# A four-layer graph network on one core: the gated layer's difference on GpSimd, and softmax sums by a 129th operand column

## The chip, the cores and the metric

The kernel runs on one core of a Trainium2 chip. The metric is the device time of one execution in microseconds (us); a lower one is better. The engines are called PE (TensorE, matrix products), PEld (its weight loads), DVE (VectorE), ACT (ScalarE), POOL (GpSimd) and SP (SyncE, which issues transfers here).

## What is computed

The input x is 64 graphs of 256 nodes with 128 features; adj is one 256x256 matrix that all graphs share. Four layers follow one another. Each normalises its input over the features, clips it at zero, and adds its result to the input. Layer 0 is a gated recurrence of five steps, layer 1 a sum of node mixings with adj and its square, layer 2 one mixing with a row norm, layer 3 an attention over node pairs:

```python
# layer 0, five times
u3 = h @ u3_w.T + u3_b
z = sigmoid(av @ w3_w.T + w3_b + u3)
r = sigmoid(av @ w4_w.T + w4_b + u3)
hv = tanh(av @ w5_w.T + w5_b + (r * h @ u5_w.T + u5_b))
h = (1.0 - z) * h + z * hv
# layer 3
pre = s1[:, :, None, :] + s2[:, None, :, :] + b_lin
h = where(pre >= 0, pre, 0.2 * pre)
e = einsum('bije,e->bij', h, a) + bias
attn = softmax(e, axis=2)
out = sigmoid(einsum('bij,bjf->bif', attn, x))
```

Here av holds adj times h twice, and in layer 3 the weights W and the bias are adj itself. Everything is in 32-bit floats.

## The kernel before

**Pairs, fronts, tiles, tails.** Two graphs form a pair (32 pairs), so that a tile [128, 2, 256] has 512 elements in each partition. For each pair a "front" (from L391) works through layers 0 to 2 and the start of layer 3: it is one long dependent chain, in which products run on PE, the Tanh and the copies out of PSUM on ACT, elementwise work on DVE, and the small inverse roots on POOL. Sigmoids are written with Tanh.

The large work is layer 3's pairwise sum and its clipping. It is cut into 128 "tiles" a pair (4096 in all), each of 128x2048 elements and called rl. A tile can be made on any of three engines: on DVE by one instruction (L703), on ACT by eight (L716), on POOL by eight (L723). DVE's tiles belong to one half of the hidden features, POOL's to the other, ACT makes either. PE scores each tile with two groups of four matmuls, once for each of the two passes of a 32-bit product (L760; each record in the profile is one of these). 13 rl tiles are in turn use.

When all 64 tiles of a block of 128 nodes have been scored, a "tail" (two for each pair) does the softmax and the weighted sum: DVE adds adj (L609), POOL adds a row term (L613, the sum sc+lin over 128x512 elements), DVE takes the negated maximum (L617), ACT takes Exp with an accumulated output as the softmax sum (L622; the accumulator is read out by an instruction of its own), PE transposes, ACT copies with a factor 0.5 to wT (L631), PE multiplies by h3, DVE inverts the sums (L643), ACT takes Tanh with that scale into o (L648), POOL finishes (L652, L653), and SP sends the result out.

**Order.** No engine chooses at run time. A planner in the kernel keeps a clock for each engine and plays the whole program through while it is being built: `ran(engine, us, ...)` advances a clock by a duration written in the code, and `yield ENGINE, since` in a front or tail says which engine has the next step and from when. At each point the engine that is free first takes a step of a tail, else of a front, else a part of a tile. What it takes is then fixed as that engine's program order, each instruction depending on the one before it. On POOL a part of a tile is two instructions, on ACT four, on DVE the whole tile. So a change in any step or duration moves the order on all engines, and also how many tiles each makes. Fronts are spread so that about two of them are under way at any time. Buffers with `tag="short"` come from a ring of 12, the tiles hT from a ring of 4, and three PSUM banks are lent out by `take()` and given back through `spare`.

**The steps that the change touches.** In a step of layer 0, pr and pv are PSUM banks with sums. ACT takes Tanh of pr for z (L437), and Tanh of pv in place, in PSUM (L440). Then:

```python
            yield DVE, t
            d = feat("d", **SHORT)
            nc.vector.tensor_sub(d, by_feature(pv[0]), hT)
            t = ran(DVE, ELEMENTS, t)
            spare.append([pv[0], t])
            yield DVE, max(t_z, clock[DVE])
            nc.vector.scalar_tensor_tensor(by_feature(pr[0]), by_feature(pr[0]), 1.0, d, op0=OP.add, op1=OP.mult)
```

These are L445 (the difference d, 160 times: 32 pairs by 5 steps) and L449 (the product); L453 forms the new hT. The norms (L365 to L376) go from DVE through POOL (L299, L300, L372) to ACT. In layer 3, h3 is the normalised input, tokens in partitions, that the weighted sum reads.

Of the kernel before, what the change touches and what calls it, by code (L numbers as in the profile page):

```python
# [8 lines left out]
F32 = mybir.dt.float32  # L9
AF = mybir.ActivationFunctionType  # L10
# [4 lines left out]
P = 128  # L15
NB = 2
# [4 lines left out]
PE, DVE, ACT, POOL = ENGINES = (mybir.EngineType.PE, mybir.EngineType.DVE, mybir.EngineType.Activation, mybir.EngineType.Pool)  # L21
# [4 lines left out]
def kernel(  # L26
# [50 lines left out]
    nc = tc.nc  # L77
    B, N, D = x.shape
    NC = N // P
# [5 lines left out]
    work = ctx.enter_context(tc.tile_pool(name="work", bufs=2))  # L85
# [9 lines left out]
    clock = dict.fromkeys((PE, DVE, ACT, POOL), 0.0)  # L95
# [4 lines left out]
    def ran(engine, us, *after):  # L100
        start = max(clock[engine], 0.0, *after)
        if engine == ACT:
            behind[0] = max(0.0, behind[0] - (start - clock[ACT])) + 0.024 * us
        clock[engine] = start + us
        return clock[engine] + SEEN[engine] + (behind[0] if engine == ACT else 0.0)
# [6 lines left out]
    spare = [[b, 0.0] for b in banks[5:]]  # L112
# [6 lines left out]
    def by_feature(b):  # L119
        return b.rearrange("p (b n) -> p b n", b=NB)  # L120

    def by_token(b):
        return b.rearrange("p (b c n) -> p b c n", b=NB, c=NC)
# [29 lines left out]
    ident = const.tile([P, P], F32, name="ident")  # L153
# [43 lines left out]
    bz, br, bh = gate_b[:, 0:1], gate_b[:, 1:2], gate_b[:, 2:3]  # L197
# [123 lines left out]
    def to_feature(pt, h):  # L321

        pt = by_token(pt)
        for b in range(NB):
            for c in range(NC):
                nc.tensor.transpose(pt[:, b, c, :], h[:, b, c, :], ident)

    def to_token(pt, ht):

# [16 lines left out]
    def tok(name, **kw):  # L346
        return work.tile([P, NB, NC, D], F32, name=name, **kw)

    def rows_of(t):
        return t.rearrange("p b c d -> p (b c) d")  # L350
# [5 lines left out]
    COPY, BIASED, TANH, ELEMENTS = 0.48, 0.58, 0.57, 0.61  # L356

    def norm(src, since, h):

        stats = work.tile([P, NB * NC, 6], F32, name="stats")  # L360
        mv = work.tile([P, NB * NC, 2], F32, name="mv")
        s, h = rows_of(src), rows_of(h)
        yield DVE, since
        for k in range(NB * NC):
            nc.vector.bn_stats(stats[:, k, :], s[:, k, :])  # L365
        for k in range(NB * NC):
            nc.vector.bn_aggr(mv[:, k, :], stats[:, k, :])
        nc.vector.tensor_scalar(mv[:, :, 0], mv[:, :, 0], -1.0, None, op0=OP.mult)  # L368
        t = ran(DVE, 1.12, since)
        yield POOL, t  # L370
        inverse_root(mv[:, :, 1], OP.add, LN_EPS)
        nc.gpsimd.tensor_mul(mv[:, :, 0], mv[:, :, 0], mv[:, :, 1])  # L372
        t = ran(POOL, 1.4, t)
        yield ACT, t
        for k in range(NB * NC):
            nc.scalar.activation(h[:, k, :], s[:, k, :], AF.Relu, bias=mv[:, k, 0:1], scale=mv[:, k, 1:2])  # L376
        return ran(ACT, 1.54, t)
# [13 lines left out]
    def front(p):  # L391
# [16 lines left out]
        for step in range(STEPS):  # L408
            yield PE, t_h, 1, lambda: "adj" in SET_UP
            b = take()  # L410
            mix_nodes(b[0], h, adj_t)
            t = ran(PE, MIX, t_h, b[1])
            yield ACT, t
            mT, t_m = copied("mT", b, t)
            yield PE, t_m, 1, lambda: "first" in SET_UP
            pr = take()
            project(pr[0], u3t, hT, stop=False)
            project(pr[0], w4t, mT, start=False)
            t = ran(PE, 2 * PROJECT, t_m, t_hT, pr[1])
            yield ACT, t, 1  # L420
            r = take()
            nc.scalar.activation(r[0], pr[0], AF.Tanh, bias=br, scale=0.5)  # L422
            t = ran(ACT, TANH, t, r[1])
            yield DVE, t
            rh = feat("rh", **SHORT)
            nc.vector.scalar_tensor_tensor(rh, by_feature(r[0]), 1.0, hT, op0=OP.add, op1=OP.mult)  # L426
            t_rh = ran(DVE, ELEMENTS, t)
            spare.append([r[0], t_rh])
            yield PE, t_rh, 1
            project(pr[0], w34, mT, start=False)  # L430
            t_z = ran(PE, PROJECT, t)
            pv = take()
            project(pv[0], w5t, mT, stop=False)
            project(pv[0], u5t, rh, start=False)
            t = ran(PE, 2 * PROJECT, t_rh, pv[1])
            yield ACT, t_z
            nc.scalar.activation(pr[0], pr[0], AF.Tanh, bias=bz, scale=0.5)  # L437
            t_z = ran(ACT, TANH, t_z)
            yield ACT, t
            nc.scalar.activation(pv[0], pv[0], AF.Tanh, bias=bh, scale=1.0)  # L440
            t = ran(ACT, TANH, t)

            yield DVE, t
            d = feat("d", **SHORT)
            nc.vector.tensor_sub(d, by_feature(pv[0]), hT)  # L445
            t = ran(DVE, ELEMENTS, t)
            spare.append([pv[0], t])
            yield DVE, max(t_z, clock[DVE])
            nc.vector.scalar_tensor_tensor(by_feature(pr[0]), by_feature(pr[0]), 1.0, d, op0=OP.add, op1=OP.mult)  # L449
            ran(DVE, ELEMENTS, t_z)  # L450
            yield DVE, clock[DVE]
            hT_new = feat("hT", bufs=4)
            nc.vector.scalar_tensor_tensor(hT_new, by_feature(pr[0]), 0.5, hT, op0=OP.mult, op1=OP.add)  # L453
            hT = hT_new
            t_hT = ran(DVE, ELEMENTS)
            spare.append([pr[0], t_hT])
            yield PE, t_hT, 1
            b = take()
            to_token(b[0], hT)
            t = ran(PE, TURN, t_hT, b[1])  # L460
            if step < STEPS - 1:
                yield ACT, t
                h = tok("h", **SHORT)
                nc.scalar.copy(h, by_token(b[0]))  # L464
                t_h = ran(ACT, COPY, t)
                spare.append([b[0], t_h])
# [76 lines left out]
        spare.append([po[0], t])  # L543


        h3 = tok("h3")
        t = yield from norm(x3, t, h3)
        yield PE, t, 1
        b = take()
# [55 lines left out]
    def tail(p, ic, pe, since, x3, h3):  # L605

        yield DVE, since
        sc = feat("sc", **SHORT)
        nc.vector.tensor_add(sc, by_feature(pe), adj_n[:, ic, :].unsqueeze(1).to_broadcast([P, NB, N]))  # L609
        t = t_pe[p * NC + ic] = ran(DVE, ELEMENTS, since)  # L610
        ops = READY[p]
        yield POOL, max(t, ops["t_lin"])
        nc.gpsimd.tensor_add(sc, sc, ops["lin"])  # L613
        t = ran(POOL, 1.05, t, ops["t_lin"])
        yield DVE, t
        nmx = work.tile([P, NB], F32, name="nmx")
        nc.vector.tensor_reduce(nmx, sc, AX.X, OP.max, negate=True)  # L617
        t = ran(DVE, ELEMENTS, t)
        yield ACT, t
        sums = work.tile([P, NB], F32, name="sums")  # L620
        for b in range(NB):
            nc.scalar.activation(sc[:, b, :], sc[:, b, :], AF.Exp, bias=nmx[:, b:b + 1], scale=1.0,  # L622
                                 accum_out=sums[:, b:b + 1])
        t_s = ran(ACT, 1.0, t)
        yield PE, t_s, 1
        b = take()
        to_token(b[0], sc)
        t = ran(PE, TURN, t_s, b[1])
        yield ACT, t
        wT = tok("wT", **SHORT)  # L630
        nc.scalar.mul(wT, by_token(b[0]), 0.5)  # L631
        t = ran(ACT, COPY, t)
        spare.append([b[0], t])
        yield PE, t, 1
        b = take()
        po = b[0][:, :NB * D].rearrange("p (b d) -> p b d", b=NB)
        for k in range(NB):
            for c in range(NC):
                side_by_side(po[:, k, :], wT[:, k, c, :], h3[:, k, c, :], c == 0, c == NC - 1)
        t = ran(PE, PRODUCT, t, b[1])  # L640
        yield DVE, t_s
        rs = work.tile([P, NB], F32, name="rs")
        nc.vector.reciprocal(rs, sums)  # L643
        t_s = ran(DVE, 0.08, t_s)
        yield ACT, max(t, t_s)
        o = work.tile([P, NB, D], F32, name="o")
        for k in range(NB):
            nc.scalar.activation(o[:, k, :], po[:, k, :], AF.Tanh, scale=rs[:, k:k + 1])  # L648
        t = ran(ACT, 0.5, t, t_s)
        spare.append([b[0], t])  # L650
        yield POOL, t
        nc.gpsimd.tensor_scalar(o, o, 0.5, 0.5, op0=OP.mult, op1=OP.add)  # L652
        nc.gpsimd.tensor_add(o, o, x3[:, :, ic, :])  # L653
        ran(POOL, 1.1, t)
        nc.sync.dma_start(out[p * NB:(p + 1) * NB, ic * P:(ic + 1) * P, :].rearrange("b p d -> p b d"), o)
        TAILED.add((p, ic))
# [215 lines left out]
```

## Time and profile before

| | us |
|---|---|
| runs | 5317.5, 5331.74, 5331.07; median 5331.07 |
| profiled execution | 5330.89, its span 5329.1 |
| mean granted TensorE clock | 0.997 of full |
| last tile ends on DVE, ACT, POOL | 5311.0, 5311.0, 5314.9 |

The span runs from the first to the last instruction of the program. In the slices of the page, all engines are at 90% or more from the second slice of 133 us to the last but one, so the run has a start of some 125 us, in which the first fronts run before any tile can be made, a long even stretch, and a short end without fronts:

```profile
PE   7999999999999999999999999999999999999998
DVE  4999999999999999999999999999999999999998
ACT  4999999999999999999999999999999999999998
POOL 1999999999999999999999999999999999999999
```

Each digit is the busy share of a fortieth of the span, in tenths. In the groups of the profile, a row gives line, engine, operation, tiles, shape and count, then busy us, the mean ns of one, and the idle time just before, with what ended it. Instructions of one engine overlap a little in the records, so a mean in a row is longer than the distance from start to start.

### The profile page before, as it was taken

The page shows a single profiled execution, that of the slowest core. Times are in us where ns is not written, and L with a number is a line of the kernel's source. Part 1 is how long each engine was busy: PE and PEld are TensorE (multiplying, and loading weights), DVE is VectorE, ACT ScalarE, POOL GpSimd, SP SyncE. Part 2 cuts the span into 40 slices and gives each one's busy share as a digit, 9 for nine tenths or more (in the row PEclk, how much of TensorE's full clock was granted, in tenths as well). Part 3 has the DMA queues.
Part 4 walks back from the last instruction along what each step waited for, and adds up shares of the span by engine and source line. Part 5 has one row for each costly group of instructions (what it writes and reads, how often), then busy time and mean ns, then how long its engine had stood idle before and what let it go on. Part 6 is the DMA issues. An engine that isn't in the chain of part 4 may idle for free.

```text
span 5329.1 us, 139126 instructions
## 1 busy us (share of the span) xinstructions
PE 5227.4 (98%) x56085; PEld 1861.5 (35%) x56085; DVE 5209.6 (98%) x4313; ACT 5132.1 (96%) x13529; POOL 5153.2 (97%) x5958
## 2 busy tenths in 40 slices
PE   7999999999999999999999999999999999999998
PEld 3333333333333333333333333333333333333332
DVE  4999999999999999999999999999999999999998
ACT  4999999999999999999999999999999999999998
POOL 1999999999999999999999999999999999999999
PEclk9999999999999999999999999999999999999999
DMA  0000000000000000000000000000000000000000
GB/s 19 7 8 5 8 7 6 8 5 8 8 5 8 7 6 8 7 6 8 5 8 7 6 8 6 6 8 7 6 8 5 8 7 6 8 5 6 6 5 4
DMA packets 60344, 37.49 MB, mean 7 GB/s; under 512 B 4528, under 2 KB 59696, under 8 KB 59696
## 3 DMA queue, kind: packets, MB, share of 16 engines
q1 hardware_dynamic: 58976, 28.59, 2.3%
q8 instruction: 438, 7.18, 0.6%
q14 instruction: 210, 1.72, 0.1%
q10 hardware_dynamic: 720, 0.00, 0.0%
HBM read 18.09 MB, written 10.49 MB: 5 GB/s over the span
## 4 chain that ended last, share of the span: by engine, by line
DVE 44%; PE 31%; POOL 15%; issue 5%; ACT 5%; DMA 0%; POOLq 0%; DVEq 0%; SPq 0%; ACTq 0%
DVE rl L703 36%; PE bank L760 20%; POOL rl L723 13%; PE bank L305 10%; ACT rl L716 4%; DVE stats L365 1%; DVE bank L449 1%; DVE d L445 1%; DVE rh L426 1%; DVE hT L453 1%; PE bank L333 1%; POOL mv L300 1%; POOL sc L613 1%; DVE mv L368 1%; DVE nmx L617 0%
## 5 line engine op out<-in xcount | busy, mean ns | idle before, releaser
L723 POOL TENSOR_SCALAR rl<-s2n,s1b 128x256 f32<-128x256 f32 x5312 | 4779.4, 953 | 9.5 <-ACT s1b L590 9.3
L703 DVE TENSOR_TENSOR rl<-s1a,bank 128x2048 f32<-128x2048 f32 x2009 | 4468.7, 2275 | 11.7 <-ACT s1a L599 11.7
L716 ACT ACTIVATE rl<-bank,s1b 128x256 f32<-128x256 f32 x11072 | 4409.4, 903 | 1.0
L760 PE MATMUL bank<-rl,win_n 128*32 128x512 f32 x21384 | 2659.7, 594 | 38.0 <-DVE rl L703 31.2
L760 PE MATMUL bank<-rl,win 128*32 128x512 f32 x11384 | 1511.8, 594 | 0.0
L760 PEld LDWEIGHTS bank<-rl,win_n 128*32 128x32 f32 x21384 | 682.5, 110 | 1512.9 <-issue 1214.9
L760 PEld LDWEIGHTS bank<-rl,win 128*32 128x32 f32 x11384 | 369.1, 110 | 749.5 <-issue 618.6
L305 PE MATMUL bank<-mT,wts 128*32 128x512 f32 x2560 | 335.0, 593 | 1.4 <-DVE d L445 0.6
L305 PE MATMUL bank<-adj_t,h 128*32 128x256 f32 x5120 | 308.5, 381 | 4.6 <-ACT h L464 3.5
L305 PEld LDWEIGHTS bank<-adj_t,h 128*32 128x32 f32 x5120 | 165.2, 110 | 174.8 <-issue 52.2
L376 ACT ACTIVATE h<-x,mv 128x128 f32<-128x128 f32 x384 | 171.3, 626 | 35.5 <-POOL mv L372 35.2
L382 ACT COPY mT<-bank 128x512 f32<-128x512 f32 x160 | 146.4, 915 | 39.0 <-PE bank L305 30.5
L305 PE MATMUL bank<-hT,wts 128*32 128x512 f32 x1280 | 168.3, 593 | 0.0
L305 PE MATMUL bank<-mT,w 128*32 128x512 f32 x1280 | 166.8, 593 | 1.3 <-ACT bank L422 1.3
L305 PE MATMUL bank<-rh,u5t 128*32 128x512 f32 x1280 | 166.6, 592 | 0.0
L422 ACT ACTIVATE bank<-bank,gate_b 128x512 f32<-128x512 f32 x160 | 150.8, 942 | 13.8 <-PE bank L305 13.5
L437 ACT ACTIVATE bank<-bank,gate_b 128x512 f32<-128x512 f32 x160 | 145.9, 912 | 16.2 <-PE bank L305 16.1
L440 ACT ACTIVATE bank<-bank,gate_b 128x512 f32<-128x512 f32 x160 | 147.3, 921 | 12.0 <-PE bank L305 10.6
L464 ACT COPY h<-bank 128x512 f32<-128x512 f32 x128 | 132.2, 1033 | 19.8 <-PE bank L333 19.8
L305 PEld LDWEIGHTS bank<-mT,wts 128*32 128x32 f32 x2560 | 82.0, 110 | 196.3 <-issue 142.4
L716 ACT ACTIVATE rl<-s2c,s1a 128x256 f32<-128x256 f32 x312 | 148.5, 891 | 0.0
L300 POOL TENSOR_TENSOR mv<-mv,minus_half 128x4 f32<-128x4 f32 x128 | 133.0, 1039 | 10.7
(113 smaller groups left out, 3204.7 us busy)
## 6 DMA issues: line engine op xcount, KB each, us to landing
xin<-in_x_dram SPq DMA_DIRECT2D x64, 128.0 KB, 2.2
lin<-row SPq DMA_DIRECT2D x32, 256.0 KB, 7.6
out_dram<-o SPq DMA_DIRECT2D x64, 128.0 KB, 1.8
row<-quarter SPq DMA_DIRECT2D x32, 64.0 KB, 1.5
w_raw<-in_L_gnn_w_w_dram SPq DMA_DIRECT2D x3, 128.0 KB, 2.7
th_raw<-in_L_gnn_Theta_dram SPq DMA_DIRECT2D x1, 320.0 KB, 3.9
adj_n<-in_adj_dram SPq DMA_DIRECT2D x1, 256.0 KB, 3.5
w_raw<-in_L_gnn_u_w_dram SPq DMA_DIRECT2D x2, 64.0 KB, 2.9
```

The costliest lines, as they stand in the source:

```text
L300: nc.gpsimd.tensor_tensor(t, t, minus_half, op=OP.pow)
L305: nc.tensor.matmul(o[g:g + 32], w[:, g:g + 32], t, start=start, stop=stop, skip_group_check=True)
L376: nc.scalar.activation(h[:, k, :], s[:, k, :], AF.Relu, bias=mv[:, k, 0:1], scale=mv[:, k, 1:2])
L382: nc.scalar.copy(c, by_feature(bank[0]))
L422: nc.scalar.activation(r[0], pr[0], AF.Tanh, bias=br, scale=0.5)
L437: nc.scalar.activation(pr[0], pr[0], AF.Tanh, bias=bz, scale=0.5)
L440: nc.scalar.activation(pv[0], pv[0], AF.Tanh, bias=bh, scale=1.0)
L464: nc.scalar.copy(h, by_token(b[0]))
L703: nc.vector.tensor_tensor(t, rows.to_broadcast(whole), ops["s2a"].unsqueeze(1).to_broadcast(whole), op=OP.min)
L716: nc.scalar.activation(t[:, g, b, :], (s2p if k else ops["s2c"])[:, b, :], AF.Relu, bias=ops["s1"][k][:, b, i:i + 1], scale=-1.0)
L723: nc.gpsimd.tensor_scalar(t[:, part, b, :], ops["s2n"][:, b, :], ops["s1"][1][:, b, i:i + 1], None, op0=OP.min)
L760: nc.tensor.matmul(pe[g * 32:(g + 1) * 32, :], w[:, k, 31 - r:63 - r], flat(t[:, g]), start=first, stop=(left[block] == 0), skip_group_che ...
```

## The change

Two edits, independent of each other:

- From the second pair on (31 pairs by 5 steps), ACT writes the Tanh of pv into d in SBUF in place of PSUM, and POOL subtracts hT from d in place. DVE no longer takes part in that difference; its next instruction, the product with pr, waits for POOL. The bank pv is given back after the Tanh. The first pair keeps the old form. In the planner the POOL step counts 1.3 us.
- In layer 3, h3 gets a 129th column of the value 2, set by POOL once a pair. The weighted sum's product is 129 columns wide, and its last column is twice the softmax sum. So Exp accumulates nothing any more, wT is copied without the factor 0.5, and the reciprocal reads the column from the PSUM bank, after the product and no longer beside it.

The other lines follow from these: the norm and the transposition take columns 0 to 127 of h. No duration of any other step is changed in the planner, apart from Exp (1.0 to 0.8) and the reciprocal (0.08 to 0.15).

```diff
             yield ACT, t
-            nc.scalar.activation(pv[0], pv[0], AF.Tanh, bias=bh, scale=1.0)
-            t = ran(ACT, TANH, t)
-
-            yield DVE, t
             d = feat("d", **SHORT)
-            nc.vector.tensor_sub(d, by_feature(pv[0]), hT)
-            t = ran(DVE, ELEMENTS, t)
-            spare.append([pv[0], t])
-            yield DVE, max(t_z, clock[DVE])
+            if p < 1:
...
+            else:
+                nc.scalar.activation(d, by_feature(pv[0]), AF.Tanh, bias=bh, scale=1.0)
+                t = ran(ACT, TANH, t)
+                spare.append([pv[0], t])
+                yield POOL, t
+                nc.gpsimd.tensor_sub(d, d, hT)
+                t = ran(POOL, 1.3, t)
+            yield DVE, max(t, t_z)
             nc.vector.scalar_tensor_tensor(by_feature(pr[0]), by_feature(pr[0]), 1.0, d, op0=OP.add, op1=OP.mult)
-            ran(DVE, ELEMENTS, t_z)
+            ran(DVE, ELEMENTS, t, t_z)
...
-        h3 = tok("h3")
+        h3 = work.tile([P, NB, NC, D + 1], F32, name="h3")
+        nc.gpsimd.memset(h3[:, :, :, D:D + 1], 2.0)
...
-            nc.scalar.activation(sc[:, b, :], sc[:, b, :], AF.Exp, bias=nmx[:, b:b + 1], scale=1.0,
-                                 accum_out=sums[:, b:b + 1])
-        t_s = ran(ACT, 1.0, t)
+            nc.scalar.activation(sc[:, b, :], sc[:, b, :], AF.Exp, bias=nmx[:, b:b + 1], scale=1.0)
+        t_s = ran(ACT, 0.8, t)
...
-        nc.scalar.mul(wT, by_token(b[0]), 0.5)
+        nc.scalar.copy(wT, by_token(b[0]))
...
-        po = b[0][:, :NB * D].rearrange("p (b d) -> p b d", b=NB)
+        po = b[0][:, :NB * (D + 1)].rearrange("p (b d) -> p b d", b=NB)
...
-        yield DVE, t_s
+        yield DVE, t
         rs = work.tile([P, NB], F32, name="rs")
-        nc.vector.reciprocal(rs, sums)
-        t_s = ran(DVE, 0.08, t_s)
-        yield ACT, max(t, t_s)
+        nc.vector.reciprocal(rs, po[:, :, D])
+        t = t_s = ran(DVE, 0.15, t)
+        yield ACT, t
```

## Prediction

> **What bounds the kernel now.** I read the page first (busy shares, slices, groups), then the windows of the steady stretch, then the waits of each engine in it, and last the timelines of single engines, which give the spacing of instructions.
>
> ```profile
> PE 5227.4 (98%) x56085; PEld 1861.5 (35%) x56085; DVE 5209.6 (98%) x4313; ACT 5132.1 (96%) x13529; POOL 5153.2 (97%) x5958
> L723 POOL TENSOR_SCALAR rl<-s2n,s1b 128x256 f32<-128x256 f32 x5312 | 4779.4, 953 | 9.5 <-ACT s1b L590 9.3
> L703 DVE TENSOR_TENSOR rl<-s1a,bank 128x2048 f32<-128x2048 f32 x2009 | 4468.7, 2275 | 11.7 <-ACT s1a L599 11.7
> L716 ACT ACTIVATE rl<-bank,s1b 128x256 f32<-128x256 f32 x11072 | 4409.4, 903 | 1.0
> ```
>
> All four engines are at 96 to 98% and three of them mostly do one thing: they make "rl" tiles that PE scores. No engine can be relieved alone, since the planner hands the freed time out again as tiles. Where the last slack lies is in the steady stretch:
>
> ```profile
> 1000.00:4000.00 3000.00, 2974.89 (x32175) 1059.43 (x32171) 2983.62 (x2457) 2937.43 (x7757) 2967.73 (x3429) 1.00 0.03 7
> ...
> POOL rn L299 <- DVE rn L531: 6.7, 3, 3.4
> ...
> DVE nmx L617 <- POOL sc L613: 5.5, 10, 1.5
> DVE x L540 <- POOL rn L300: 4.5, 8, 0.8
> ...
> ACT h L376 <- POOL mv L372: 25.4, 26, 2.7
> ACT sc L622 <- DVE nmx L617: 8.2, 7, 2.3
> ```
>
> The first line is the window of 3000 us, with busy us of PE, PEld, DVE, ACT, POOL; below are waits of POOL (one line, that is all there are), DVE and ACT in it. POOL waits for others 6.7 us in 3000, while DVE (10 us) and ACT (25 us) wait mainly for POOL. So POOL, slightly behind its plan, paces the rest; DVE is next (99.5% busy), PE third. POOL's other idle time, 32.3 - 6.7 = 25.6 us, is no wait but a fixed gap:
>
> ```profile
> 1999.21 0.93 POOL L723 TENSOR_SCALAR rl<-s2n,s1b 128x256 f32<-128x256 f32 x1
> 2000.23 0.23 POOL L299 TENSOR_SCALAR mv<-mv 128x4 f32<-128x4 f32 x1
> 2000.54 1.04 POOL L300 TENSOR_TENSOR mv<-mv,minus_half 128x4 f32<-128x4 f32 x1
> 2001.66 0.20 POOL L372 TENSOR_TENSOR mv<-mv 128x4 f32<-128x4 f32 x1
> 2001.83 16.21 POOL L723 TENSOR_SCALAR rl<-s2n,s1b 128x256 f32<-128x256 f32 x18
> 2017.97 1.32 POOL L613 TENSOR_TENSOR sc<-sc,lin 128x512 f32<-128x512 f32 x1
> 2019.24 14.41 POOL L723 TENSOR_SCALAR rl<-s2n,s1b 128x256 f32<-128x256 f32 x16
> 2033.73 0.41 POOL L652 TENSOR_SCALAR o<-o 128x256 f32<-128x256 f32 x1
> ```
>
> About 0.08 us stands ahead of L299, L300, L372 and L652, and none ahead of L613. From the same lines come POOL's true prices, start to start: 18 tile instructions in 16.14 us, 0.897 each (the 953 ns of the page overlap); L613 takes 2019.24 - 2017.97 = 1.27 us.
>
> **What the Trainium skill says.** "GPSIMD Engine Reference", section 3.1 (side-by-side cycle accounting): two inputs share one read port, some 2.6 cycles an element at 1.2 GHz, so 512 elements give an estimated 1.11 us plus dispatch; L613, that very shape, shows 1.27. The same page, Specifications, has GpSimd and VectorE contend only where VectorE is in a two-port mode or reads two SBUF inputs; the VectorE tile instruction L703 has one input in a PSUM bank, and the sums L613 spread only from 1.26 to 1.40 us beside it, so I add no contention. "Perfetto Trace Analysis" (opening note) calls matmul busy time a bad metric; the 98% of PE is therefore not my bound. "ScalarE: Activation LUTs", section on what happens in an ACTIVATE, calls PSUM the faster destination; the Tanh into PSUM (L440) and the biased copies into SBUF (L590) both space at about 0.58 us here, so at most 0.03 us is at stake.
>
> **The change part by part.** The order of the built kernels gives counts, and no time is in it. Of the 4096 tiles DVE makes 2045 instead of 2009 (+36), ACT 1416 instead of 1423 (-7, 56 instructions), POOL 635 instead of 664 (-29, 232 instructions). The last front still ends about 181 scored tiles before the end of PE's order, so the shape of start and end is kept. 155 differences (31 pairs by 5 steps) move.
>
> ```profile
> L445 DVE TENSOR_TENSOR d<-bank,hT 128x512 f32<-128x512 f32 x160 | 108.5, 678 | 27.8 <-ACT bank L440 27.8
> L613 POOL TENSOR_TENSOR sc<-sc,lin 128x512 f32<-128x512 f32 x64 | 84.9, 1327 | 2.8 <-DVE sc L609 2.8
> L622 ACT ACTIVATION_READ_ACCUMULATOR sc<-sc,nmx 128x1 f32 x128 | 49.7, 421 | 0.0
> L643 DVE RECIPROCAL rs<-sums 128x2 f32<-128x2 f32 x64 | 10.3, 160 | 1.2 <-ACT sc L622 1.2
> ```
>
> - POOL: -232 x 0.897 = -208 us; +155 x 1.26 = +195; 32 memsets of a 128x4 column at 0.1 each (the page's memsets are 99 to 205 ns), +3. Net -10 us. Unknown is the fixed gap ahead of the new difference: L613, which also waits on another engine, has none, L652 has 0.08; I take none, and 155 x 0.08 = 13 us is the upper bound, which gives +3.
> - DVE: in DVE's timeline five L703 in a row take 11.06 us, the last one 2.28, so (11.06 - 2.28)/4 = 2.195 each, and L445 spaces at 0.60 alone and 0.72 where L449 follows at once and waits for it; 0.65 as mean. -155 x 0.65 = -101; +36 x 2.195 = +79; the reciprocal reads a strided PSUM column, 0 to 0.1 us dearer, 64 x 0.06 = +4. Net -18 us.
> - ACT: an L716 spaces at 0.36: -56 x 0.36 = -20. The accumulator reads show 421 ns but cost 0.10 of spacing (2022.28 to 2022.38 in ACT's timeline): -128 x 0.10 = -13. Tanh into SBUF, 0 to 0.03 dearer: up to +4. Net about -30 us.
> - PE: 512 groups of four, with one column in 129 more, at about 0.11 us a group: under half a us. The bank pv comes free before the difference rather than after it, a small help that I cost at nothing because banks cause no visible wait of PE's.
> - New waits. POOL's difference waits for ACT's Tanh; behind it on POOL stand tile instructions. POOL works late, so the Tanh should be long done (as for L652, one long wait at the end apart): 0 to 5 us. DVE's product now waits for POOL; behind it stand L703 tiles that PE needs. Bounds: 0.01 each as L445 had on ACT (0.4 us in this window), 0.2 each as L540 has on POOL (4.5 us for 18 groups of 32 overall). The plan holds 1.3 us for an instruction of 1.26, while for L613 it holds 1.05 against 1.27, which is why L617 waits; so I take 0.07: +11 us on DVE. Against DVE's -18 that stays covered.
> - The reciprocal behind PE instead of behind Exp lengthens each tail by a hop to DVE, with a tile of 2.2 us ahead of it at worst. Tile work covers it, except for the last tail: +0.3 us less 0.2 of accumulator reads.
> - Start: pair 1's five steps are each about 0.7 us longer; its work is queued among pair 0's, while engines idle anyway (PE 80 of 100 us in 50 to 150). 0 to +4 us, taken as 0 to 1.
>
> Sum: the pacing engine loses 10 us of work, DVE about 7 after its waits, ACT 30, PE nothing. POOL's 10 us is the likeliest gain, less a little for start and new waits: -9 us. The profiled run took 5330.9 us (span 5329.1 and 1.8 around it), and the median of the runs is 5331.1, so the forecast on either is 5322.
>
> **The rivals.**
> - More than POOL's share comes back. In tiles, DVE gains (101 - 4)/2.195 = 44, ACT (13 - 4)/2.9 = 3, POOL loses 195/7.18 = 27: net +20 tiles, and the three together make 1/2.195 + 1/2.9 + 1/7.18 = 0.94 a us, so 21 us. With ACT's waits for POOL shrunk by a few more, 5307. For it: DVE and ACT both get lighter. Against it: POOL waits for nothing now, so it must itself become lighter, and does by 10 only.
> - Slower: the new POOL hand-off becomes DVE's wait. Mechanism: DVE's product stands in a fixed order behind a POOL instruction that runs late; DVE, 99.5% busy, can't make it up. At 0.35 us a wait, the price of ACT's wait L376 on POOL (25.4 us over about 74 norms in the window), DVE gets +54 - 18 = +36 us, and 5365; at 0.25, +21 and 5350. It decides from about 0.12 us a wait, where DVE's relief is spent; from 0.22 it is a slowdown that can be measured. Against it: POOL's planned duration fits the new instruction.
> - Nothing reaches the end: the gap of 0.08 is paid on POOL (+3) or PE's own limit holds: 5331 to 5334. PE in the steady stretch is 99.2% busy by the window, and its load is not changed at all.
>
> **How the numbers follow.** POOL's share alone, 5308 to 5336: 0.48. Full redistribution: 0.22. Slower through the hand-off: 0.20. No effect: 0.10. A measurement of this kernel tells 0.3% (16 us, so 5315 and 5347) from no change; its three runs spread over 14 us. From the cases: faster 0.21 and the quick end of the first case 0.08, so 0.29; slower 0.19, nearly the whole second rival; same 0.52. The range leaves out the far halves of both rivals: 5300 to 5350. Both signs hold much of the chance, so the likeliest case's own range is 5308 to 5336.
>
> **What would show it.** The new difference should stand at 1.25 to 1.35 us in POOL's groups, with no gap ahead of it; POOL's waits should stay under some 10 us in the steady stretch; the product on DVE should show under 15 us of waiting for it in the whole run; the accumulator row should be gone; the 32x129 products should cost as before. Wrong it would be if that DVE wait exceeds 30 us, if POOL starts to wait for Tanh, if the difference takes clearly more than 1.3 us beside VectorE, or if the last tile, now within 4 us on DVE, ACT and POOL, ends unevenly.

## The result and the profile after

The changed kernel takes 5311.5 us (median of 6 runs, 5298.85 to 5313.18) against 5331.1 before: ratio 0.9961, 95% interval 0.9951 to 0.9972. It is faster by 0.4%, a little more than the 0.3% from which the prediction counts a change as one.

The time of either kernel lies at one of two values some 13 us apart (before 5318 or 5331, after 5299 or 5311.5), the gain is about 19 us at both, and since the first profile of the kernel before is one of 5331 and that of the changed kernel one of 5299, 13 of the 32 us between their spans (5329.1 and 5297.1) are not the change.

The page of the changed kernel, busy us of each engine, then groups (busy us, mean ns, idle before):

```profile
PE 5206.2 (98%) x56085; PEld 1854.6 (35%) x56085; DVE 5187.0 (98%) x4194; ACT 5084.2 (96%) x13345; POOL 5128.7 (97%) x5913
...
L730 POOL TENSOR_SCALAR rl<-s2n,s1b 128x256 f32<-128x256 f32 x5080 | 4564.2, 930 | 10.2 <-ACT s1b L599 9.0
L710 DVE TENSOR_TENSOR rl<-s1a,bank 128x2048 f32<-128x2048 f32 x2045 | 4543.1, 2276 | 11.3 <-ACT s1a L608 11.3
...
L454 POOL TENSOR_TENSOR d<-d,hT 128x512 f32<-128x512 f32 x155 | 200.8, 1295 | 65.8 <-ACT d L450 65.8
```

The difference has gone to POOL (L454, 1295 ns in the records), POOL has 232 tile instructions fewer, and no accumulator read is left. In the even stretch, 1000 to 4000 us, busy time of PE, PEld, DVE, ACT and POOL:

```profile
1000.00:4000.00 3000.00, 2980.58 (x32256) 1062.29 (x32252) 2988.12 (x2395) 2915.24 (x7664) 2969.99 (x3420) 1.00 0.03 7
```

In the same stretch, all waits of POOL (the first line) and of DVE, with total, times and longest:

```profile
POOL rn L299 <- DVE rn L539: 4.5, 4, 3.1
...
DVE nmx L626 <- POOL sc L622: 3.2, 7, 0.8
DVE bank L457 <- POOL d L454: 2.0, 6, 0.5
DVE x L548 <- POOL rn L300: 1.9, 4, 0.7
```

The pattern is that of before: POOL waits for hardly anything, DVE is 99.6% busy, ACT has become idler (85 us in 3000 in place of 63). The new hand-off costs DVE 2.0 us in 3000. The timeline of POOL gives the price of the difference and shows no gap ahead of it:

```profile
2001.16 1.29 POOL L622 TENSOR_TENSOR sc<-sc,lin 128x512 f32<-128x512 f32 x1
2002.42 5.40 POOL L730 TENSOR_SCALAR rl<-s2n,s1b 128x256 f32<-128x256 f32 x6
2007.78 1.29 POOL L454 TENSOR_TENSOR d<-d,hT 128x512 f32<-128x512 f32 x1
2009.04 3.61 POOL L730 TENSOR_SCALAR rl<-s2n,s1b 128x256 f32<-128x256 f32 x4
2012.73 0.41 POOL L659 TENSOR_SCALAR o<-o 128x256 f32<-128x256 f32 x1
```

From 2007.78 to the next start is 1.26 us, the same as for L622 above it; ahead of L659 stands the gap of 0.08.

### The profile page after: what moved, and what is told of

It reads as the page before. It is cut to its first block, busy times and chain, and to the rows that moved or that the text cites. A ratio compares the mean times of both kernels' runs of the same rounds, so it can differ in the third digit from the quotient of the medians.

```text
span 5297.1 us, 138355 instructions
## 1 busy us (share of the span) xinstructions
PE 5206.2 (98%) x56085; PEld 1854.6 (35%) x56085; DVE 5187.0 (98%) x4194; ACT 5084.2 (96%) x13345; POOL 5128.7 (97%) x5913
## 4 chain that ended last, share of the span: by engine, by line
PE 41%; DVE 29%; POOL 19%; ACT 5%; issue 5%; DMA 0%; POOLq 0%; ACTq 0%; DVEq 0%; SPq 0%
PE bank L767 27%; DVE rl L710 25%; POOL rl L730 16%; PE bank L305 12%; ACT rl L723 4%; PE bank L333 1%; POOL d L454 1%; DVE hT L461 1%; DVE bank L457 1%; DVE stats L365 1%; POOL mv L300 1%; DVE rh L426 1%; POOL sc L622 0%; PE bank L326 0%; DVE x L548 0%
## 5 line engine op out<-in xcount | busy, mean ns | idle before, releaser
L730 POOL TENSOR_SCALAR rl<-s2n,s1b 128x256 f32<-128x256 f32 x5080 | 4564.2, 930 | 10.2 <-ACT s1b L599 9.0
L710 DVE TENSOR_TENSOR rl<-s1a,bank 128x2048 f32<-128x2048 f32 x2045 | 4543.1, 2276 | 11.3 <-ACT s1a L608 11.3
L723 ACT ACTIVATE rl<-bank,s1b 128x256 f32<-128x256 f32 x11304 | 4491.7, 890 | 2.3 <-PE bank L767 0.5
L767 PE MATMUL bank<-rl,win 128*32 128x512 f32 x11328 | 1483.7, 593 | 0.0
L454 POOL TENSOR_TENSOR d<-d,hT 128x512 f32<-128x512 f32 x155 | 200.8, 1295 | 65.8 <-ACT d L450 65.8
L437 ACT ACTIVATE bank<-bank,gate_b 128x512 f32<-128x512 f32 x160 | 157.7, 986 | 19.8 <-PE bank L305 19.6
L450 ACT ACTIVATE d<-bank,gate_b 128x512 f32<-128x512 f32 x155 | 151.8, 979 | 9.7 <-PE bank L305 9.7
L422 ACT ACTIVATE bank<-bank,gate_b 128x512 f32<-128x512 f32 x160 | 144.7, 904 | 16.6 <-PE bank L305 12.2
L300 POOL TENSOR_TENSOR mv<-mv,minus_half 128x4 f32<-128x4 f32 x128 | 133.0, 1039 | 10.7
```

The costliest lines, as they stand in the source:

```text
L300: nc.gpsimd.tensor_tensor(t, t, minus_half, op=OP.pow)
L450: nc.scalar.activation(d, by_feature(pv[0]), AF.Tanh, bias=bh, scale=1.0)
L454: nc.gpsimd.tensor_sub(d, d, hT)
L710: nc.vector.tensor_tensor(t, rows.to_broadcast(whole), ops["s2a"].unsqueeze(1).to_broadcast(whole), op=OP.min)
L723: nc.scalar.activation(t[:, g, b, :], (s2p if k else ops["s2c"])[:, b, :], AF.Relu, bias=ops["s1"][k][:, b, i:i + 1], scale=-1.0)
L730: nc.gpsimd.tensor_scalar(t[:, part, b, :], ops["s2n"][:, b, :], ops["s1"][1][:, b, i:i + 1], None, op0=OP.min)
```

## The experiments

The experiments ran in three sets, each on another chip: e1 to e4, e5 to e8, e9 to e12. Ratios are against runs of the kernel before on the same chip, whose medians were 5318.3, 5318.8 and 5318.0 us. "Theory A" is that POOL paces the even stretch, "theory B" that all makers share the load and no engine paces alone.

**Each edit alone (e1, e2).** e1 is the kernel before with only this:

```diff
-            nc.scalar.activation(pv[0], pv[0], AF.Tanh, bias=bh, scale=1.0)
...
-            nc.vector.tensor_sub(d, by_feature(pv[0]), hT)
...
+                nc.scalar.activation(d, by_feature(pv[0]), AF.Tanh, bias=bh, scale=1.0)
...
+                nc.gpsimd.tensor_sub(d, d, hT)
```

> The difference on POOL from the second pair on, softmax sums as before. Tile counts: DVE 2046, ACT 1415, POOL 635. Theory A (POOL paces the even stretch, so the time follows POOL's own work): POOL loses 232 x 0.897 = 208 us and gains 155 x 1.25 = 194, so -14 us: ratio 0.997, nearly all of the whole change's gain. Theory B (all makers share the load, and what counts is the sum of what is freed, 44 - 27 = 17 tiles at 0.94 tiles a us): -18 us, ratio 0.9966. If the softmax part carries the gain instead: ratio 0.999 to 1.001.

Measured: 5303.2 us, ratio 0.9971 (0.9960 to 0.9982), 15 us less. e2 is the changed kernel with the old difference on DVE everywhere, so only the 129th column:

> The 129th column alone, difference on VectorE as before. Tile counts: DVE 2006, ACT 1426, POOL 664 as before. Theory A: POOL has the same tiles and 32 memsets of 0.05 us more, so 0 to +2 us, ratio 1.000. Theory B: ACT is freed of 128 reads of 0.10 us (13 us, 4 tiles), -3 to -5 us, ratio 0.999. If this part carries the gain: ratio 0.996 to 0.997.

Measured: 5316.1 us, ratio 0.9996 (0.9988 to 1.0004): not to be told from nothing. So the difference carries most of the gain. These two don't separate A from B, since both foretold nearly the same.

**What does a microsecond on each engine cost (e5, e6, e7)?** The changed kernel's program order is kept on all engines, and 155 instructions that the planner doesn't know of are put on one of them, after each difference, in the fronts from the second pair on. Their output is read by nobody.

```diff
+            if p > 0:
+                nc.gpsimd.tensor_scalar(scratch, adj_n[:, 0, 0:P], 1.0, None, op0=OP.mult)   # e5
+                nc.scalar.copy(scratch, adj_n[:, 0, 0:P])                                     # e6
+                nc.vector.tensor_copy(scratch, pr[0][:, 0:P])                                 # e7
             yield DVE, max(t, t_z)
```

> The changed kernel, its order untouched, with 155 more POOL instructions that the planner doesn't know of: a 128x128 product with a constant, after each difference, into a tile that nobody reads. Estimated 0.30 us and 0.08 of gap each, 155 x 0.38 = 59 us of POOL. Theory A (POOL paces): nearly all of it comes out, +45 to +60 us. Theory B (no engine paces alone): a third, about +20 us.

> As the run before, but the 155 additional instructions are 128x128 copies on ACT, SBUF to SBUF, estimated at 0.16 to 0.25 us, 25 to 40 us in all. Theory A: ACT has 125 us of idle in 4600, so 0 to +5 us. Theory B: a third, about +10 us.

> As the run before, but the 155 additional instructions are 128x128 copies on VectorE, PSUM to SBUF, estimated at 0.2 to 0.26 us, 31 to 40 us in all. Theory A: VectorE is the second, with 16 us of idle in 4600, so the time grows by what exceeds that, +10 to +25 us. Theory B: a third, about +12 us.

What one costs is read from the timelines of POOL (e5), ACT (e6) and DVE (e7), start to start:

```profile
2004.15 1.29 POOL L455 TENSOR_TENSOR d<-d,hT 128x512 f32<-128x512 f32 x1
2005.53 0.54 POOL L458 TENSOR_SCALAR scratch<-adj_n 128x128 f32<-128x128 f32 x1
2006.04 3.61 POOL L733 TENSOR_SCALAR rl<-s2n,s1b 128x256 f32<-128x256 f32 x4
```

```profile
2008.16 0.36 ACT L458 COPY scratch<-adj_n 128x128 f32<-128x128 f32 x1
2008.35 1.65 ACT L726 ACTIVATE rl<-bank,s1b 128x256 f32<-128x256 f32 x4
```

```profile
2018.62 0.28 DVE L458 COPY scratch<-bank 128x128 f32<-128x128 f32 x1
2018.82 0.16 DVE L653 RECIPROCAL rs<-bank 128x2 f32<-128x2 f32 x1
```

On POOL the piece shown takes 2006.04 - 2004.15 = 1.89 us from L455 to the next tile instruction; without L458 that was 1.26, so 0.63 more. A gap of 0.09 ahead of L458 is in it, which most such pieces lack: the mean of the 123 of them between 500 and 4900 us is 1.81, so 0.55 more. On ACT it is 0.19, on DVE 0.20. The changed kernel took 5299.15 us (e10), so:

| | added work | measured | more than e10 | share of it that comes out |
|---|---|---|---|---|
| POOL (e5) | 155 x 0.55 = 85 us | 5374.0 | 74.9 | 88% |
| ACT (e6) | 155 x 0.19 = 29 us | 5300.8 | 1.7 | 6% |
| DVE (e7) | 155 x 0.20 = 31 us | 5321.2 | 22.0 | 71% |

e10 ran on another chip, where the kernel before was 0.8 us quicker, so up to 0.8 us of each difference may be the chip's. The even stretch agrees: a pair takes 165.04 us in e5, 162.59 in e6 and 163.32 in e7 against 162.63 in e10 (how a pair is timed stands at e3 and e11), which is 88% of the work added there on POOL, nothing on ACT and 69% on DVE.

The POOL instruction was dearer than estimated (0.30 and a gap), so the time beyond the expectation is more work, not a larger share. Theory B (a third for each) falls for a given order. With the order held no tile can change its engine, so these runs don't tell what a planner that hands out freed time would gain. POOL paces, ACT has room, and DVE stands so close behind POOL that most of what is added there comes out too: it had 12 us of idle in 3000, some 16 in the even stretch, and 31 us were put on it; 15 were to come out, 22 did. In e5 the waits for POOL grow in the same stretch, here DVE's and ACT's:

```profile
DVE x L551 <- POOL rn L301: 17.6, 16, 2.3
DVE nmx L629 <- POOL sc L625: 11.3, 20, 1.3
DVE bank L460 <- POOL d L455: 11.1, 21, 1.3
...
ACT h L377 <- POOL mv L373: 68.4, 47, 3.2
```

The wait of the product on POOL is 11.1 us there in place of 2.0: that is the rival of the forecast, at its work once POOL really is late.

**Relieving POOL (e4, e8).** POOL's small steps are dearer than the planner holds them to be. The planner is told the real durations, in the kernel before (e8) and in the changed one (e4, there the difference at 1.25 too):

```diff
-        t = ran(POOL, 1.4, t)      # norm
+        t = ran(POOL, 1.72, t)
...
-        t = ran(POOL, 1.25, t)     # row norm
+        t = ran(POOL, 1.44, t)
...
-        t = ran(POOL, 1.05, t, ops["t_lin"])   # sc + lin
+        t = ran(POOL, 1.25, t, ops["t_lin"])
...
-        ran(POOL, 1.1, t)          # end of the tail
+        ran(POOL, 1.31, t)
```

> The kernel before with the planner told POOL's real durations (norm 1.72 for 1.4, row norm 1.44 for 1.25, tail sum 1.25 for 1.05, tail end 1.31 for 1.1). POOL makes 656 tiles in place of 664, ACT 1427 for 1423, DVE 2013 for 2009. Theory A: POOL 57 us lighter; VectorE, with 22 us of idle in 4600 and 9 us more work, takes over: -10 to -15 us, ratio 0.9975. Theory B: no change, ratio 1.000.

> The whole change with the planner told POOL's real durations (norm 1.72 in place of 1.4, row norm 1.44 for 1.25, tail sum 1.25 for 1.05, tail end 1.31 for 1.1, difference 1.25 for 1.3). POOL makes 627 tiles in place of 635, ACT 1423 for 1416, DVE 2046 for 2045. Theory A: POOL is 57 us lighter and no longer late, so the next engine paces: VectorE has 16 us of idle in 4600, so 10 to 20 us less than the changed kernel, about 5295, ratio 0.993. Theory B, or a bound on PE: 0 to -4 us against the changed kernel, ratio 0.9955.

Measured: e8 5309.4 us, ratio 0.9983 (0.9976 to 0.9990), 9 us less than before on that chip. e4 5288.45 us, ratio 0.9943 (0.9930 to 0.9955), 10.7 us less than e10. Both go the way of theory A, at or just under the lower end of what it gave. DVE was not the pacer: in e4 it makes one tile more than in the changed kernel, and the time still falls. The window of e4 shows the hand-over:

```profile
1000.00:4000.00 3000.00, 2989.82 (x32377) 1066.90 (x32373) 2995.30 (x2401) 2936.87 (x7727) 2945.39 (x3392) 1.00 0.03 7
```

And the two longest of POOL's waits in it:

```profile
POOL sc L622 <- DVE sc L618: 11.2, 17, 1.4
POOL mv L299 <- DVE mv L367: 9.8, 18, 1.1
```

Now POOL waits for DVE, and DVE has under 5 us of idle in 3000.

**Relieving DVE too (e12).** On top of e4:

```diff
-        t = ran(DVE, 1.12, since)   # norm
+        t = ran(DVE, 1.4, since)
...
-            done = ran(DVE, 2.2, since)   # a tile
+            done = ran(DVE, 2.195, since)
```

> The changed kernel with the planner told the real durations of POOL (as in the run with 627 POOL tiles) and of VectorE (norm 1.4 for 1.12, tile 2.195 for 2.2). VectorE makes 2039 tiles, ACT 1428, POOL 629. Theory A, with VectorE the pacer once POOL is relieved: against the run with POOL's durations alone VectorE loses 15 us, ACT gains 15 of its 100 us of idle, POOL gains 14 of about 44: -8 to -15 us, 5275 to 5281, ratio 0.992. If PE or the hand-offs bound by then: 5285 to 5290, ratio 0.994.

Measured: 5268.6 us, ratio 0.9906 (0.9893 to 0.9920), 20 us less than e4 and more than foretold. It beats both kernels. In its window DVE waits for 1 us and POOL for some 11 us in all, and PE is 99.9% busy:

```profile
1000.00:4000.00 3000.00, 2997.03 (x32464) 1070.49 (x32460) 2994.39 (x2407) 2956.78 (x7783) 2962.87 (x3411) 1.00 0.03 7
```

The expected 8 to 15 us are there: in the traces the stretch from the score of tile 512 to that of tile 4000 is 13.4 us shorter than in e4. The remainder of their distance stands before tile 512 (6.6 us) and after tile 4000 (0.8), where e4 was longer than e10 by 3.3 and 2.3 us. Why the corrected durations lay out the start so differently was not tried, nor whether PE bounds the kernel now.

**The start (e3, e11).** The exemption of the first pairs is moved by one in either direction:

```diff
-            if p < 1:
+            if p < 0:    # e3: no pair is exempt
+            if p < 2:    # e11: pairs 0 and 1 are exempt
```

> The whole change, and the first pair's five differences on POOL too; same tile counts as the changed kernel (2045, 1416, 635). Pair 0's chain is bare in the start: POOL's 1.25 us instead of VectorE's 0.60, and one hop more, so 0.7 to 0.8 us a step: first score 3 to 4 us later than in the changed kernel's profile (121 us), time +3 to +4 us, ratio against before about 0.9968. If the start has slack there, no difference: 0.996.

> The changed kernel, but pairs 0 and 1 both keep the difference on VectorE. Tile counts as in the changed kernel (2045, 1416, 635). If the second pair's differences on POOL are what brings the first score from about 125 to 121 us: first score at 124 to 126 here and 3 to 4 us more than the changed kernel, ratio 0.997. If that came from the softmax part or by chance: 121, and no more time.

Measured: e3 5309.3 us (ratio 0.9984, 0.9977 to 0.9990; its runs lie from 5308 to 5312), 10 us more than e10. e11 5303.3 us (0.9972, 0.9961 to 0.9982), 4.1 us more. The first score on PE starts at 122.1 us in e10, at 125.7 in e11 and at 132.9 in e3, and after it the traces of e10 and e11 have the same 162.63 us a pair (24 pairs, tile 512 to tile 3584 scored). So the whole distance between these two is in the start. (Two traces of the changed kernel, 121.1 and 122.1, show how far one kernel's first score moves by itself.) The waits of DVE in the first 130 us, in the kernel before and in the changed one:

```profile
DVE d L445 <- ACT bank L440: 27.4, 10, 5.1
DVE rh L426 <- ACT bank L422: 17.1, 7, 8.3
```

```profile
DVE bank L457 <- POOL d L454: 16.6, 5, 6.5
DVE d L446 <- ACT bank L443: 14.2, 5, 3.6
DVE rh L426 <- ACT bank L422: 13.6, 8, 3.8
```

In the start two fronts share engines that are mostly idle, in a fixed order. Pair 1's Tanh is now waited for on POOL and no longer on DVE. That this frees pair 0's steps behind it on DVE fits the waits, but is argued, not shown. What is shown is that the second pair's differences on POOL bring 4 us, and that the first pair's, put there too, cost 10. e3 missed its expectation by a factor of three: the hop is no more than 0.8 us a step, yet DVE waits for POOL 33.8 us in 8 pieces in that start.

**The two kernels again (e9, e10).** Both as they were, on the third chip.

> The kernel before, once more with a profile, beside the changed kernel on one chip, since in its first profile a POOL tile instruction spaces at 0.898 us and in all later profiles, of whatever kernel, at 0.896. Theory A (POOL paces): with 0.896 here the even stretch must be shorter by 0.25% than in the first profile, 162.9 us a pair instead of 163.3, and the run takes about 5318 us. If POOL's pace and the run's time aren't tied: 163.3 again with either spacing.

> The changed kernel, timed on the chip of the experiments. Expected 5299 us, ratio 0.9963; even stretch 162.6 us a pair. Theory A asks for about 0.4 us a pair between this and the run before (12 us in all, POOL's net of 232 tile instructions and 155 differences), the remainder in the start and the end.

Measured: e10 5299.15 us, ratio 0.9964 (0.9950 to 0.9978), even stretch 162.63 us a pair. e9 is one run of 5330.8 us, although 10 of the 11 other runs of the kernel before on that chip took 5317 to 5319. So my expectation for e9, the quicker pace and 5318, missed, and no trace of the kernel before at 5318 is at hand. e2, with the same 664 tiles on POOL, stands in for it. The rows of POOL's tile instructions in e9 and e2:

```profile
L723 POOL TENSOR_SCALAR rl<-s2n,s1b 128x256 f32<-128x256 f32 x5312 | 4779.3, 934 | 9.0 <-ACT s1b L590 8.8 <-issue 0.2
```

```profile
L723 POOL TENSOR_SCALAR rl<-s2n,s1b 128x256 f32<-128x256 f32 x5312 | 4767.1, 931 | 9.5 <-ACT s1b L592 9.1 <-issue 0.4
```

Busy time divided by count is 0.8997 us a tile instruction in e9, as in the first profile (4779.4 us), and 0.8974 in e2. A pair of the even stretch takes 163.35 us in e9, 163.30 in the first profile and 162.99 in e2. DVE's tile instructions space at 2.197 us in all three, so it is not that everything runs slower. The 12 us by which POOL is busier are close to the 13 between the two values of the kernel before. So POOL's pace and the time go together, as theory A has it. That the two values are this and nothing else is not shown, since no kernel was traced at both, and what changes the pace is open.

## Why the prediction was right, and by how much it missed

The forecast was 5322 and "same" the likeliest; 5311.5 lies in the range and within the likeliest case's own 5308 to 5336, but it is just on the faster side of 0.3%, to which 0.29 was given. A gain of 9 was foretold, and about 19 came. The pacer and its share of the gain were right; the other 8 us, from the start and the last tiles, were foretold at nothing, and that 5311.5 still lies in the range is owed to its width. By steps:

- **The bound.** That POOL paces is shown by e5 (88% of added POOL time comes out), e6 (at most 6% of ACT's) and the relief in e4 and e8. That DVE is next is shown by e7 and e4. PE's 98% was rightly not taken for the bound: e12 puts more matmuls into the same window.
- **POOL's sum, -10.** Right. The difference spaces at 1.26 as taken, without the gap, and a memset adds about 0.05 where 0.1 was taken; -208 + 195 + 2 = -11. e2 and e10 differ in the first edit alone, whose sum without the memsets is -13. Between their traces the stretch from the first score to that of tile 4000 is shorter by 13.0 us, the start by 3.3 and the end by 0.7. DVE's work differs between these two by about as much (39 tiles more, 155 differences less, -15), so that alone doesn't single out POOL; e4, e5 and e8 do.
- **New waits, +11 on DVE in all, covered.** For the even stretch mis-sized on the safe side: 2.0 us in 3000, or 0.02 each where 0.07 was taken. The slower rival needed 0.12. (Its two times are also mis-added: 5331 + 36 and + 21 are 5367 and 5352, not 5365 and 5350.) In the whole run it is 19.9 us, over the 15 that were given as a sign, with 16.6 of them in the start. There POOL also waits for the Tanh, which was taken at 0 to 5 us: 64.5 us in five waits up to 130 us, and 1.3 after that. Both signs failed for the start, which the prediction had looked at only as a longer chain.
- **The start, taken as 0 to +1.** The mis-sized term: it brought -4 (e11 against e10). I priced the hop of pair 1's chain and left out that its differences also go out of DVE's queue; that this is the cause is, as said, not shown.
- **The second edit, -30 on ACT and nothing in time.** Nearly right: e2 alone shows nothing beyond its interval; e10 is 4.0 us below e1, their intervals overlap. From the score of tile 4000 to the end of the span the traces have 120.5 us in e1, 115.8 in e10 and 116.5 in e2, so these few us stand in the last tiles. Whether they come from the lighter ACT or from how the planner lays out the end is open; the planner's correction in e8, without this edit, shortens the end likewise (116.8, against 119.5 in the kernel before).

Sum: -11, -4, -4, which is -19. The rival of full redistribution gave 5307 and came nearer than the forecast (4.5 us off, where that was 10.5 off), but by luck: it puts the whole gain into the even stretch, 18 us for the first edit alone, where e2 and e10 show 13, POOL's own sum.

## What to carry to other kernels

When a planner keeps all engines near 98%, ask which engine waits for nobody and whom the others wait for: what a change takes from that engine is its gain, and a check is to put known work on each engine in turn with the order held. Here, of the work put on the idlest engine at most 6% came out as time, on the pacer 88%, and the second was so near that it took over at once. Here moving work was worth less than telling the planner true durations: two corrected DVE numbers and a handful on POOL gave 30 us on top of the change, the change itself 19.

## What the runs showed of the hardware that was not expected

- POOL's pace is not the same in each execution: the same 5312 tile instructions are busy for 4779 us (first profile, e9) or 4767 (e2), a quarter of a per cent, and the time of this POOL-paced kernel goes with it. The cause is open.
- A one-operation product of 128x128 by a constant on POOL took 0.54 us (e5), and a tile instruction with one operation 0.9 for 128x256, while L659, two operations in place on 128x256, takes 0.41. What makes it so (second operation, pointer or constant, in place) was not tried; for tiles that are made on POOL it would matter.
- An accumulator read that shows 421 ns on ACT took some 0.1 us of its time (from its start to the next start 0.09 in the median, in the kernel before).
- The Tanh of 128x512 spaces at 0.57 us (median) on ACT both into SBUF (L450) and into PSUM (L437) in the changed kernel, so moving its output cost ACT nothing that shows.
